# A chunk's product with the state ahead of the output projection of the chunk before, and small products in a group's waits

## The chip, the cores and the metric

The kernel runs on one core of one Trainium2 chip. A core has five engines, each with its own in-order queue: TensorE (PE in the profile; its weight loads are shown as PEld), VectorE (DVE), ScalarE (ACT), GpSimd (POOL) and SyncE (SP), which issues most DMAs. Matmuls write PSUM[...]. The metric is the time of one execution on the device, in microseconds (us); the median of several runs is compared.

## The reference, cut to what matters

```python
x = x + attn_a(layernorm(x))      # state-space mixer, 16 heads of 64, state 64
x = x + ffn(layernorm(x))
x = x + attn_b(layernorm(x))      # state-space mixer, 64 heads of 16, state 128
x = x + ffn(layernorm(x))         # the same ffn weights again
```

x is 4 x 1024 x 512, float32. Each mixer projects x to a gate z, to the channels h, B, C and to a step dt; h, B and C go through a causal convolution of four taps and a silu. Then, with a decay a = A*dt per head,

```python
state = exp(a_t) * state + (dt_t * h_t) outer B_t
y_t   = C_t . state + D * h_t
out   = rmsnorm_and_gate(y, z) @ out_proj
```

The kernel computes the recurrence by chunks of 128 positions. Inside a chunk y is a masked product, exp(segment sums of a) * (C B^T), times dt*h; what came before enters as C times the state at the chunk's start (`from_state`); then the state is brought on (`to_state`).

## The kernel before

The program is mixer A, ffn, mixer B, ffn, one behind the other. In a mixer the 4 x 1024 positions are 32 chunks of 128, eight to a batch row, and two chunks make a group (16 groups). A group's input projections, convolutions, gates and steps are the function `front`, a generator that yields after each of its 17 (A) or 18 (B) pieces: eight `gate` pieces (a `pz` product each) and nine (A) or ten (B) `convolve` pieces (a `pc` product each, ScalarE's `u` at L470 and three VectorE operations at L474 that read it). Two chunks of a group are worked off by `chunk` while the pieces of the next group's `front` are mixed in.

All four compute engines are under a manual schedule: instructions stand on each engine in the order in which the Python code issues them. The mixing is done by the loop at the end of `mixer`. Each `yield` of `chunk` names a time that is added to `due`; while `due` is positive, the next piece is issued and its own time (1.75 for a gate, 1.9 for a convolution) taken off. In the last group of a mixer there are no pieces. Functions put into `later_on` are issued after the next piece. The list `small` holds short TensorE steps (transposes, dt products, and the 13 steps of the next chunk's `prologue`: five in `sums_of`, eight in `turn`, two of which end in a VectorE product `hdt`, L713); `large` issues one of them after each big matmul, and `finish` issues what is left when a chunk needs it. `turn` also puts `skip` (four ScalarE scalings of h, L727) into `later_on`.

A chunk begins so, in program order:

1. `finish(f)`: what is left of its prologue (`misc`, `tph`; Gm, ea, Bt, hdt).
2. `fold` of the chunk before: two VectorE sums of its squares (L971, L972).
3. `decays(0)`: twelve short matmuls into four PSUM tiles `seg` (L789, L799), and four ScalarE exps that read them into `L` (L806).
4. `next(last, None)`, the first step of the `tail` of the chunk before: the output projection `pout` (eight products of 512 columns, L670) and the sum of squares `ssq` (L672), which needs `fold`. Its readers (`leave`: the copy at L679 and VectorE's `rs` at L680) go to `later_on`.
5. `from_state()`, unless the chunk is the first of its batch row: two products `po` (L847) of C with the state, and two VectorE products `yo` (L851) that read them.
6. On GpSimd `hdr` (L919) and the scaling of the state (L928), which waits for `po`.

Then come the weighing of `L` with Gm (`weigh`, L813), the transposes of `yo` into `py` (L860), the products of `L` with dt*h into `py` (`inner`, L829), `close_y` (L878 to L885) and `to_state` (`pst` L898, L907 or L909).

The profile counts a float32 product as two matmul instructions: `pout` is sixteen, `po` four. All the tiles that `mm(...)` makes (`pc`, `pz`, `pd`, `tpx`, `misc`, `tph`, `seg`, `pout`, `ssq`, `po`, `pst`, `pcs`) share the pool `p_mm`, seven PSUM buffers of one bank each; `py` has the eighth bank. A new tile waits until the last reader of the tile that had its buffer is done.

Of the kernel before, what the change touches and what calls it, by code (L numbers as in the profile page):

```python
# [72 lines left out]
def hybrid_kernel(  # L73
# [114 lines left out]
    def lay_constants():  # L188
        eye = ident.rearrange("p (r w) -> p r w", w=32)
        for i, at in enumerate(  # L190
            [slice(2 + h + 10 * lo, 7 + h + 10 * lo, 4) for lo in (0, 1) for h in range(HB)]
            + [slice(10 * lo, 10 * lo + 2) for lo in (0, 1)]
            + [slice(20, 21)]
        ):
            nc.vector.tensor_reduce(flags[:, i : i + 1], eye[:, :, at], mybir.AxisListType.XY, ALU.add)
        nc.vector.scalar_tensor_tensor(
            heads4, flags[:, HB : 2 * HB], 1.0 / LO_SCALE, heads4, ALU.mult, ALU.add
        )
        nc.vector.scalar_tensor_tensor(
            first2, flags[:, 2 * HB + 1 : 2 * HB + 2], 1.0 / LO_SCALE, first2, ALU.mult, ALU.add  # L200
        )
        for past in pasts:
            nc.vector.tensor_scalar_mul(
                past.rearrange("p t s -> p (t s)"), first2.to_broadcast([P, SETS * P]), -1.0
            )
            nc.vector.tensor_scalar(past[:, :, 64:], past[:, :, 64:], row20, None, ALU.add)

    def lay_flags(sets):
        for upto in sums:
            for t in sets:  # L210
                nc.vector.tensor_copy(upto[:, t], heads4.unsqueeze(2).to_broadcast([P, HB, P]))
                nc.vector.scalar_tensor_tensor(
                    upto[:, t, :, :64],
                    row20.unsqueeze(1).to_broadcast([P, HB, 64]),
                    MASKED,
                    upto[:, t, :, :64],
                    ALU.mult,
                    ALU.add,
                )
# [27 lines left out]
    def mixer(m, in_w, conv_w, conv_b, dt_bias, A_log, Dv, norm_w, out_w, src, dst, first, stats, last_steps={}):  # L247
# [14 lines left out]
        def state_at(half):  # L262
            return (slice(half * N, half * N + N), slice(0, 512)) if SH == 2 else (slice(0, N), slice(half * 512, half * 512 + 512))

        stack = ExitStack()
        with stack:
# [6 lines left out]
            def mm(name):  # L273
                return p_mm.tile([P, 512], F32, tag="mm", name=name)
# [69 lines left out]
            small = []  # L344
# [286 lines left out]
            def heads_of(ap):  # L631
                return ap.rearrange("p (h d) -> p h d", d=HD)

            def over_head(ap, parts, n):

                return ap.unsqueeze(2).to_broadcast([parts, n, HD])

            def packed(t, n):

                return t[:, n, 0::2, :]  # L640
# [122 lines left out]
            def chunk(f, c, following):  # L763
# [8 lines left out]
                last = state["tail"]  # L772
# [9 lines left out]
                def decays(t):  # L782

                    sg = [mm(f"seg_{tag}_{t}_{r}").rearrange("p (h l) -> p h l", h=HB) for r in range(4)]

                    for r in range(4):
                        for q in range(2):
                            at = slice(64 * q, 64 * q + 64)
                            nc.tensor.matmul(  # L789
                                sg[r][at, :, at],  # L790
                                ident16[at, at],
                                later[at, at].unsqueeze(1).to_broadcast([64, HB, 64]),
                                start=True,
                                stop=False,
                                skip_group_check=True,
                            )
                    for r in range(4):
                        rows = slice(32 * r, 32 * r + 21)
                        nc.tensor.matmul(  # L799
                            sg[r], past[rows, t, :], upto[rows, t], start=False, stop=True, skip_group_check=True  # L800
                        )
                    Ls = []
                    for r0 in (0, 2):
                        L = wk.tile([P, 2, HB, P], F32, tag="L", name=f"L_{tag}_{t}_{r0}", bufs=LB)
                        for r in range(2):
                            nc.scalar.activation(L[:, r], sg[r0 + r], AF.Exp)  # L806
                        Ls.append(L)
                    return Ls
# [32 lines left out]
                def from_state():  # L841

                    pos = []
                    for half in range(2):
                        rows, hsl = state_at(half)
                        po = mm(f"po_{tag}_{half}")
                        nc.tensor.matmul(po, Cc[rows, cols], state["S"][rows, hsl], start=True, stop=True)  # L847
                        pos.append(po)
                    for half, po in enumerate(pos):
                        tmp = wk.tile([P, 512], F32, tag="yo", name=f"yo_{tag}_{half}", bufs=2)  # L850
                        nc.vector.tensor_mul(  # L851
                            heads_of(tmp), heads_of(po), over_head(el[:, half * HALF : (half + 1) * HALF], P, HALF)
                        )
                        tmps.append(tmp)
# [56 lines left out]

                state.pop("fold", lambda: None)()
                L0 = decays(0)
                next(last, None)
                if not begin:
                    from_state()
                if not end:
                    hdr = wk.tile([P, E], F32, tag="hdr", name=f"hdr_{tag}")
                    nc.gpsimd.tensor_mul(  # L919
                        hdr.rearrange("p (n u d) -> p n u d", u=HC, d=HD),  # L920
                        packed(hdt, slice(0, NH // HC)),
                        er.rearrange("p (n u) -> p n u", u=HC).unsqueeze(3).to_broadcast([P, NH // HC, HC, HD]),
                    )
                    if begin:
                        Sp = wk.tile([P, SW], F32, tag="S", name=f"S_{tag}")
                    else:
                        Sp = state["S"]
                        nc.gpsimd.tensor_mul(heads_of(Sp), heads_of(Sp), over_head(et, P, NH // SH))  # L928
# [52 lines left out]
            with tc.manual_schedule(  # L981
                engines={
                    mybir.EngineType.PE,
                    mybir.EngineType.DVE,
                    mybir.EngineType.Activation,
                    mybir.EngineType.Pool,
                }
            ):
                fs = [Group(*groups[0]), Group(*groups[1])]
                for _ in norm(fs[0], None):  # L990
                    pass
                if first:
                    lay_constants()
                    lay_flags(range(TS))
                weighing = weigh_rows()
                for at, _ in enumerate(front(fs[0], fs[1])):
                    catch_up()
                    if at >= 6:
                        next(weighing, None)
                for _ in weighing:  # L1000
                    pass
                lay_sums(fs[0], 0)
                if first:
                    lay_flags(range(TS, SETS))
                for n in range(len(groups)):
                    if n + 2 < len(groups):
                        fs.append(Group(*groups[n + 2]))
                    f, ahead, behind = (fs + [None, None])[n : n + 3]
                    pieces = front(ahead, behind) if ahead is not None else iter(())
                    due = 0.0  # L1010
                    for c in range(GC):
                        following = (f, c + 1) if c + 1 < GC else (None if ahead is None else (ahead, 0))
                        for us in chunk(f, c, following):
                            due += us
                            while due > 0.0:
                                waiting, later_on[:] = later_on[:], []
                                piece = next(pieces, None)
                                for step in waiting:
                                    step()
                                if piece is None:  # L1020
                                    break
                                due -= piece
                            catch_up()
                    for _ in pieces:
                        catch_up()
                state.pop("fold")()
                for _ in state["tail"]:
                    catch_up()
# [438 lines left out]
```

## Time and profile before

| | |
|---|---|
| time, median of 3 runs | 3053.41 us (3053.19 to 3053.58) |
| the profiled execution: time, and its span | 3044.65 us, 3042.9 us |
| mean granted TensorE clock | 0.963 of full |
| mixer A, about | 60 to 1160 us: TensorE busy 1043.3 of 1100 |
| first ffn, about | 1160 to 1416 us |
| mixer B, about | 1416 to 2810 us: TensorE busy 1259.2 of 1394 |
| second ffn | the rest |
| busy share of the span | PE 91%, DVE 68%, ACT 41%, POOL 24% |

How to read it: one execution is traced. A row of the timeline is a start and a length in us, the engine, the line of the kernel, the operation, the tile written and the tiles read, the shape, and how many instructions the row merges; in brackets stands how long the engine idled before the row, and what ended that. A row of the waits is who waited for whom: us in total, times, the longest.

### The profile page before, as it was taken

What the parts mean: (1) busy time and instruction counts of PE and PEld (TensorE: products, weight loads), DVE (VectorE), ACT (ScalarE), POOL (GpSimd) and SP (SyncE); (2) the same over time, 40 slices, a digit from 0 to 9 for tenths busy, and PEclk for the clock granted to TensorE, in tenths of its full rate; (3) what the DMA queues carried; (4) which work ended last, traced back from release to release, by engine and by line L of the source; (5) the groups of instructions that cost most, each with busy time, mean ns of one, the idle gap of its engine ahead of it and who ended that gap; (6) DMA issues with size and microseconds to landing.
All of it is one profiled execution on the core that took longest, in us unless ns stands there. A gap on an engine that the chain in (4) does not pass through costs nothing. (4 is left out here: it accounts for less than half of the span.)

```text
span 3042.9 us, 46127 instructions
## 1 busy us (share of the span) xinstructions
PE 2767.9 (91%) x17156; PEld 1789.5 (59%) x17156; DVE 2081.7 (68%) x4417; ACT 1261.8 (41%) x2874; POOL 720.3 (24%) x839
## 2 busy tenths in 40 slices
PE   7999999999999988999999899999888888898986
PEld 5666666666666653456666666666555565564332
DVE  5667666766666662477777687776787777875368
ACT  3334433334333332355444444444444444443245
POOL 1222122122212221351111112212222222212057
PEclk8999999999999999999999999999999999998999
DMA  3000000000000015430000000000000000001423
GB/s 117 14 19 16 16 16 17 24 17 17 16 17 22 10 68 205 154 102 10 17 20 20 13 20 18 13 17 21 22 25 21 20 23 20 13 11 72 170 88 110
DMA packets 92959, 124.25 MB, mean 41 GB/s; under 512 B 38728, under 2 KB 42328, under 8 KB 92736
## 3 DMA queue, kind: packets, MB, share of 16 engines
q1 hardware_dynamic: 80960, 98.23, 10.0%
q10 hardware_dynamic: 9792, 16.82, 1.5%
q0 software_dynamic: 1984, 6.26, 0.6%
q8 instruction: 136, 2.23, 0.3%
q14 instruction: 87, 0.71, 0.1%
HBM read 84.54 MB, written 36.72 MB: 40 GB/s over the span
## 5 line engine op out<-in xcount | busy, mean ns | idle before, releaser
L347 PE MATMUL pc_b<-xnT_b,w_in_b 128*128 128x259 f32 x1280 | 355.7, 408 | 25.1 <-DVE S_b L909 21.9
L813 DVE TENSOR_TENSOR L_b<-L_b,Gm_b 128x1024 f32<-128x1024 f32 x256 | 308.7, 1247 | 2.9 <-ACT L_b L806 2.9
L347 PE MATMUL pz_a<-xnT_a,w_in_a 128*128 128x256 f32 x1024 | 296.5, 408 | 2.9 <-ACT Bt_a L756 2.3
L347 PE MATMUL pc_a<-xnT_a,w_in_a 128*128 128x259 f32 x1152 | 299.1, 394 | 0.0
L806 ACT ACTIVATE L_b<-seg_b 128x512 f32<-128x512 f32 x512 | 263.6, 603 | 74.0 <-PE seg_b L799 74.0
L347 PE MATMUL pz_b<-xnT_b,w_in_b 128*128 128x256 f32 x1024 | 291.4, 397 | 2.9 <-ACT xnT_b L436 2.9
L474 DVE SCALAR_TENSOR_TENSOR u_b<-pc_b,cw_b,u_b 128x256 f32<-128x256 f32 x480 | 231.5, 482 | 79.8 <-ACT u_b L470 68.3
L347 PEld LDWEIGHTS pc_b<-xnT_b,w_in_b 128*128 128x128 f32 x1280 | 229.3, 198 | 92.7 <-DVE S_b L909 25.4
L474 DVE SCALAR_TENSOR_TENSOR u_a<-pc_a,cw_a,u_a 128x256 f32<-128x256 f32 x432 | 208.2, 482 | 73.6 <-ACT u_a L470 63.3
L1205 PE MATMUL g_ps<-gw,xnT_f 128*128 128x512 f32 x512 | 246.9, 619 | 9.6 <-DMA gw<-in_L_ffn_gate_w 4.2
L829 PE MATMUL py_b<-L_b,hdt_b 128*32 128x128 f32 x4096 | 165.7, 299 | 97.6 <-DVE L_b L813 96.5
L670 PE MATMUL pout_a<-w_out_a,h_a 128*128 128x512 f32 x512 | 240.2, 613 | 0.0
L670 PE MATMUL pout_b<-w_out_b,h_b 128*128 128x512 f32 x512 | 235.7, 604 | 0.0
L347 PEld LDWEIGHTS pc_a<-xnT_a,w_in_a 128*128 128x128 f32 x1152 | 200.9, 190 | 58.5 <-DVE rs_a L685 11.4
L882 POOL TENSOR_TENSOR h_b<-h_b,z_b 128x256 f32<-128x256 f32 x128 | 90.8, 730 | 509.5 <-ACT sq_b L881 509.5
L347 PEld LDWEIGHTS pz_a<-xnT_a,w_in_a 128*128 128x128 f32 x1024 | 172.3, 195 | 55.0 <-ACT out_a L679 14.4
L347 PEld LDWEIGHTS pz_b<-xnT_b,w_in_b 128*128 128x128 f32 x1024 | 174.5, 194 | 48.8 <-issue 26.0
L829 PEld LDWEIGHTS py_b<-L_b,hdt_b 128*32 128x32 f32 x4096 | 112.6, 117 | 147.7 <-DVE L_b L813 60.5
L1205 PEld LDWEIGHTS g_ps<-gw,xnT_f 128*128 128x128 f32 x512 | 93.2, 196 | 122.1 <-issue 113.5
L881 ACT ACTIVATE sq_b<-h_b 128x256 f32<-128x256 f32 x128 | 47.9, 417 | 262.5 <-DVE h_b L878 262.5
L670 PEld LDWEIGHTS pout_a<-w_out_a,h_a 128*128 128x128 f32 x512 | 93.3, 192 | 100.1 <-issue 96.3
L670 PEld LDWEIGHTS pout_b<-w_out_b,h_b 128*128 128x128 f32 x512 | 92.3, 190 | 99.5 <-issue 95.7
(321 smaller groups left out, 4919.7 us busy)
## 6 DMA issues: line engine op xcount, KB each, us to landing
d<-in_L_ffn_d_w SPq DMA_DIRECT2D x4, 2048.0 KB
x_f<-xa SPq DMA_DIRECT2D x32, 256.0 KB
xb<-x_b ACTq DMA_DIRECT2D x32, 256.0 KB
x_f<-xb SPq DMA_DIRECT2D x32, 256.0 KB
x_a<-in_L_attn_a_x SPq DMA_DIRECT2D x30, 256.0 KB
xa<-x_a ACTq DMA_DIRECT2D x30, 256.0 KB
out<-x_f SPq DMA_DIRECT2D x22, 256.0 KB
xf<-x_f SPq DMA_DIRECT2D x20, 256.0 KB
```

Of the source, the lines that this page charges most:

```text
L347: nc.tensor.matmul(*args, **kw)
L474: nc.vector.scalar_tensor_tensor(u, ps[:, k : k + GT], cw[:, j, k : k + 1], u, ALU.mult, ALU.add)
L670: nc.tensor.matmul(pout, f.hs[e // 2][:, e % 2, cols], w_out[:, e, :], **on)
L806: nc.scalar.activation(L[:, r], sg[r0 + r], AF.Exp)
L813: nc.vector.tensor_mul(Lr, Lr, Gm.unsqueeze(1).to_broadcast([P, 2 * HB, P]))
L829: nc.tensor.matmul(py[cg * CT : (cg + 1) * CT, e % 4, :], hdt[:, h // HC, u : u + HC, :], Ls[half][:, r, hq, :], start=not started[cg], st ...
L881: nc.scalar.activation(sr, yh, AF.Square)
L882: nc.gpsimd.tensor_mul(yh, yh, zs[half * 2 + r][:, :, cols])
L1205: nc.tensor.matmul(ps, xnT[:, k, :], gw[:, k, :], start=(k == 0), stop=(k == KD - 1 and not bias_on_pe))
```

## The change

The call of `from_state` moves ahead of `next(last, None)`: on TensorE the chunk's four `po` instructions come ahead of `pout` and `ssq` of the chunk before, and their tiles are allocated ahead of those. On VectorE, ScalarE and GpSimd this move leaves the order as it is, since `tail`'s first step issues nothing there by itself.

In the loop at the end of `mixer`, when no piece is left, one step of `small` is issued at a time and 0.35 taken off `due`, until `due` is used up or `small` is empty. This can happen throughout the last group, and behind the last piece of any other.

```diff
                 state.pop("fold", lambda: None)()
                 L0 = decays(0)
-                next(last, None)
                 if not begin:
                     from_state()
+                next(last, None)
                 if not end:
                     hdr = wk.tile([P, E], F32, tag="hdr", name=f"hdr_{tag}")
...
                                 for step in waiting:
                                     step()
                                 if piece is None:
+
+                                    if small:
+                                        small.pop(0)()
+                                        due -= 0.35
+                                        continue
                                     break
                                 due -= piece
```

## The prediction

> **What bounds the kernel now.** I read the page first: TensorE is busy 91% of the span, the next engine 68%. An edit that moves TensorE work is therefore worth what it does to TensorE's own waits, and the second view to read is the table of waits. Call a group's first chunk even and its second odd; times are us from the span's start.
>
> ```profile
> PE 2767.9 (91%) x17156; PEld 1789.5 (59%) x17156; DVE 2081.7 (68%) x4417; ACT 1261.8 (41%) x2874; POOL 720.3 (24%) x839
> ```
> ```profile
> DVE yo_a L851 <- PE po_a L847: 124.7, 28, 8.6
> DVE yo_b L851 <- PE po_b L847: 122.0, 55, 7.4
> ...
> PE ssq_a L672 <- DVE sq_a L972: 28.8, 14, 2.7
> ```
>
> VectorE sits 247 us waiting for the product with the state (po), because po stands behind the output projection (pout, then ssq) on TensorE. That is what the edit moves. But VectorE's idle time counts only where TensorE later waits for VectorE. TensorE's own wait at this place is the third line: ssq waits for fold (L972) in 14 odd chunks of mixer A. The third view is one such chunk, engine by engine. TensorE:
>
> ```profile
> 512.38 0.40 PE L799 MATMUL seg_a<-upto,past 21*128 21x512 f16 x4
> 512.70 6.28 PE L670 MATMUL pout_a<-w_out_a,h_a 128*128 128x512 f32 x14
> 521.16 0.35 PE L672 MATMUL ssq_a<-ones,sq_a 128*128 128x1 f32 x2 [2.19 <-DVE sq_a L972]
> 521.38 1.10 PE L670 MATMUL pout_a<-w_out_a,h_a 128*128 128x512 f32 x2
> 522.32 0.28 PE L672 MATMUL ssq_a<-ones,sq_a 128*128 128x1 f32 x2
> 522.53 2.08 PE L847 MATMUL po_a<-S_a,Cc_a 64*128 64x512 f32 x4
> 524.53 3.09 PE L347 MATMUL pz_a<-xnT_a,w_in_a 128*128 128x256 f32 x10
> ```
>
> ScalarE and VectorE in the same stretch:
>
> ```profile
> 512.58 1.52 ACT L419 ACTIVATE xn_a<-x_a,mv_a 128x512 f32<-128x512 f32 x2 [2.69 <-DVE mv_a L417]
> ...
> 514.62 0.54 ACT L470 ACTIVATE u_a<-pc_a,cb_a,cw_a 128x256 f32<-128x256 f32 x1
> ...
> 517.07 2.04 ACT L806 ACTIVATE L_a<-seg_a 128x512 f32<-128x512 f32 x4
> ```
> ```profile
> 515.19 1.52 DVE L474 SCALAR_TENSOR_TENSOR u_a<-pc_a,cw_a,u_a 128x256 f32<-128x256 f32 x3 [2.26 <-ACT u_a L470]
> ```
>
> What to see: when TensorE reaches pout at 512.70, ScalarE is about 4 us behind. It has not yet read the last two convolution results, and it reads the four seg banks only from 517.07. Today pout covers that lag.
>
> **Why the order of allocation matters.** All these tiles live in a pool of seven PSUM buffers, handed out in the order in which they come free. At the start of an odd chunk of A the four segs hold four, and three convolution results the rest. In the program of before, pout takes the first one's buffer (read by 511.1), ssq the second one's (read until 515.19+1.52 = 516.71; it asks 7 us later, so this costs nothing), and po0, po1 take seg0's and seg1's. The edit swaps the claims: po0 takes the first, po1 the second, pout seg0's, ssq seg1's. TensorE runs in order, so everything behind po1 and pout (pout's 16 instructions, ssq, the gates) waits with them.
>
> **Odd chunks of A (15 with pieces left).** After the edit: po0 512.70 to 513.27 (half of the 1.13 us that an undisturbed po_a takes); po1 from 516.71 to 517.3; pout when the first exp ends, 517.07+0.58 = 517.65. pout and ssq take 7.41 without a wait (1101.00 to 1108.41 in another chunk), so the gates start at 525.06 against 524.53. The 2.19 wait on fold is gone (ssq now comes after 523, fold ended at 521.0), and two new waits of 3.4 and 0.4 have taken its place. The same lines in the other chunks: the first exp ends 3.9 us (3 chunks), 4.5 (1), 4.9 (7) or 5.4 (3) after the segs, 4.75 in the mean; the gates would start 4.75+7.45 = 12.2 after the segs, where they started 11.45 in the mean: 14 x 0.76 = 10.7, and 0.5 for the 15th, whose exp ends after 1.5. **+11.2 us** at unchanged clock.
>
> **The clock.** TensorE's granted clock falls to half after a poor stretch of 3.41 us:
>
> ```profile
> 447.40:450.81 3.41, 2.32 (x6) 0.76 (x4) 3.20 (x12) 2.36 (x5) 0.00 (x0) 1.00 0.00 0
> 450.81:454.23 3.42, 2.32 (x10) 1.20 (x10) 0.92 (x2) 0.58 (x1) 0.00 (x0) 1.00 0.00 0
> ```
> ```profile
> 519.09:522.50 3.41, 1.34 (x6) 0.89 (x6) 1.78 (x6) 0.02 (x1) 0.00 (x0) 1.00 0.00 0
> 522.50:525.92 3.42, 3.42 (x8) 1.69 (x9) 1.28 (x3) 0.58 (x1) 1.09 (x2) 0.50 0.00 0
> ```
>
> (Columns: length, then busy time of PE, PEld, DVE, ACT, POOL, the clock, DMA.) The same 2.18 us wait, split over two stretches (PE busy 2.32 of 3.41 in each), costs nothing; inside one (1.34) it halves the next. Seven of the 14 waits did so. The price is 0.95 up to po's end (chunks with and without, same wait) plus 0.66 on the next ten gate matmuls (3.09 against 2.43): 1.6 per halved stretch, and 3.0 where two follow each other (after the 2.73 waits). The new idle time is 3.4+0.4 within 4.4 us; however it falls, one stretch holds more than half idle. I take one halved stretch in ten chunks and two in four: 10x1.6+4x3.0 = 28. Of before's seven, the part up to po's end is in the 11.45 already; 7x0.66 = 4.6 is still to be taken off. **+23 us**. Bounds: none at all (-4.6) and two everywhere (+37).
>
> [...] The row above halves after 2.07 us idle of 3.41, so I follow the row.
>
> **Even chunks (12 in each mixer).** The exps follow the segs at once (first ended 0.6 after them in A, 0.3 in B), po finds the buffers of misc and of the first transposes free, and pout comes 1.1 (A) or 1.9 us (B) later, with its buffer free. TensorE executes the same work without a wait: 0. VectorE gets its two yo (0.69 each) earlier, but its next work waits for the dt projection behind pout: 0.
>
> **Odd chunks of B.** In nine the first exp ends at 0.6 or so: no new wait. VectorE saves 1.4 us, but z, ahead of L's weighing, waits for the gate's tanh within 0.2 us of where it ran: -0.5 in all. In the six where the last step of the first ffn is done too (from 2098 on), it ends 2.6 to 4.8 after the segs (3.7 in the mean) and po takes 1.9: pout starts 1.8 later than it could, against 0.3 to 1.7 of ssq wait removed. The gates come 1.1 later; TensorE's later waits on VectorE (0.5 to 1.5 each) give half back. 5 x 0.55 = 2.7 (the sixth already ran at half clock), and clock about 2.3 (1.8 us of idle falls into one stretch about 45% of the time). **+5**, between 0 and +12.
>
> **Small products at the end of a group.** Costs per chunk sum to 33.0 in A and the pieces to 31.1, so 1.9/0.35 gives six of the nine remaining prologue steps; in B 0.6 gives two. They stood next on TensorE anyway, so its order is unchanged: 0. In A four ScalarE scalings (0.31 each) now go ahead of the exps, by up to 0.9 us; whether pout's buffer is then seg0's or the second transpose's, I can't tell from the trace: 0 to 0.4 in 15 chunks. I take 0 (free within 0.5 of the segs by the transposes' row), +6 for the range.
>
> **Last groups.** Without pieces, the 13 steps now run in chunk 6 instead of as a burst ahead of chunk 7. They fall into waits such as this one:
>
> ```profile
> 1117.47 1.09 PE L860 MATMUL py_a<-ident,yo_a 128*128 128x128 f32 x4 [4.27 <-DVE h_a L878]
> ```
>
> The burst took 4.2 us in A (1120.39 to 1124.59, at half clock) and 2.0 in B. Against it, Gm (0.28) waits for its products ahead of the weighing of L on VectorE, up to 1 us, and the two hdt products (0.68 each) join its queue. I take **-3** for both, -6 to +1 for the range.
>
> **Queues.** Nothing moved issues a DMA: lay_sums stands ahead of the last yield and a Group's loads after it. SP is passed by nothing. On POOL the state's scaling (1.04 or 1.93) can start 7 us earlier, but POOL idled 218 and 192 us for it: 0.
>
> **Sum**: 11.2+23+5-0.5-3 = +36. The profiled execution took 3044.65 (span 3042.9), 8.8 under the median of the three runs; the sum is a difference on that execution, put on the median: 3053.4+36 = 3089.
>
> **Rivals.** (1) *The swap works as named; faster.* If pout finds a free buffer at +1.1 us, ssq meets fold 1.1 us later and each of the 14 waits shrinks by 1.1: -16; a wait of 1.1 halves no clock, up to -11 more; with the last groups, about 3028. It decides where pout's buffer comes free earlier than 1.1 us after the segs. For it: 28.8 us of ssq wait and 247 of VectorE are there. Against: L806 at 517.07. (2) *New waits, no loss of clock*: 11.2-4.6+2.7-3.5 = +6, 3059. Against: seven halvings after shorter waits. (3) *Worse*: two halved stretches in every chunk and the 0.4 in A's even ones: about 3115. (4) *Nothing*: gains and waits cancel within 0.2% (6 us, about what a measurement can tell from no change).
>
> **Chances**: main case (3072 to 3108) 0.70; rival 2 0.10, half of it within 0.2%; rival 1 0.10; rival 3 0.07; rival 4 0.03. Faster 0.10, same 0.08, slower 0.82. The range 3060 to 3112 leaves out rival 1, most of rival 3 and half of rival 2.
>
> **What would show it.** Right: the ssq wait of 28.8 us near 0; in A, TensorE waiting some 3 us at po or pout in 14 chunks, released by VectorE's u (L474) and ScalarE's L (L806); more half-clock stretches between 90 and 1080; yo's wait on po mostly gone without a gain. Wrong: pout directly behind po in A's odd chunks, or fewer half-clock stretches.

## The result, and the profile after

| | before | after |
|---|---|---|
| median of the runs compared | 3053.49 us (3053.19 to 3058.24, 4 runs) | 3096.69 us (3094.42 to 3099.74, 4 runs) |
| the profiled execution: time, span | 3044.65, 3042.9 | 3095.69, 3094.0 |
| mean granted TensorE clock | 0.963 | 0.953 |

The change makes the kernel slower: the ratio is 1.0138, with a 95% interval of 1.0121 to 1.0156, or 43 us.

The page after, engine by engine (busy us, share of the span, instructions):

```profile
PE 2813.3 (91%) x17156; PEld 1808.2 (58%) x17156; DVE 2086.6 (67%) x4417; ACT 1260.0 (41%) x2874; POOL 722.7 (23%) x839
```

The instruction counts are those of before. VectorE and ScalarE are as busy as they were (2081.7 and 1261.8 before); TensorE, with the same 17156 instructions, is busy 45 us longer (2767.9 before): not more work, but work at a lower clock, or work that no longer runs side by side. Both turn up below. The table of waits after (who waited for whom: total us, times, longest):

```profile
PE po_a L847 <- DVE u_a L474: 40.9, 14, 3.6
...
PE pout_b L670 <- ACT L_b L806: 10.1, 6, 2.0
```
```profile
DVE v_b L511 <- PE pd_b L503: 151.1, 32, 7.7
DVE v_a L511 <- PE pd_a L503: 148.0, 32, 7.0
...
DVE rs_a L680 <- PE ssq_a L672: 70.7, 18, 6.0
```

The row of `ssq` waiting for `fold`, 28.8 us, is gone, and so are VectorE's 247 us of waiting for `po`. In their place TensorE waits for VectorE's `u`, in 14 chunks again, and in mixer B for ScalarE's exps. VectorE's idle time was not saved, it moved to later waits for TensorE: at `v` (L511) for the dt projection 299 us in all, where it was 171 before, and at `rs` for `ssq`. An odd chunk of mixer A, TensorE:

```profile
538.29 0.40 PE L799 MATMUL seg_a<-upto,past 21*128 21x512 f16 x4
538.62 1.12 PE L847 MATMUL po_a<-S_a,Cc_a 64*128 64x512 f32 x2
542.77 1.09 PE L847 MATMUL po_a<-S_a,Cc_a 64*128 64x512 f32 x2 [3.04 <-DVE u_a L474]
543.80 7.97 PE L670 MATMUL pout_a<-w_out_a,h_a 128*128 128x512 f32 x14
551.61 0.28 PE L672 MATMUL ssq_a<-ones,sq_a 128*128 128x1 f32 x2
551.75 1.10 PE L670 MATMUL pout_a<-w_out_a,h_a 128*128 128x512 f32 x2
552.69 0.28 PE L672 MATMUL ssq_a<-ones,sq_a 128*128 128x1 f32 x2
552.83 2.41 PE L347 MATMUL pz_a<-xnT_a,w_in_a 128*128 128x256 f32 x10
```

VectorE and ScalarE in the same stretch:

```profile
541.11 1.52 DVE L474 SCALAR_TENSOR_TENSOR u_a<-pc_a,cw_a,u_a 128x256 f32<-128x256 f32 x3 [2.26 <-ACT u_a L470]
```
```profile
538.49 1.52 ACT L419 ACTIVATE xn_a<-x_a,mv_a 128x512 f32<-128x512 f32 x2 [2.69 <-DVE mv_a L417]
...
542.99 2.04 ACT L806 ACTIVATE L_a<-seg_a 128x512 f32<-128x512 f32 x4
```

What to see: po1 stands still until VectorE has read the second convolution result (541.11+1.52 = 542.63), and `pout`, which covered this lag before, stands behind it. ScalarE's lag is `xn` (L419) at the very start of the chunk: it waits 2.69 us for VectorE's `mv`, then takes 1.52, and everything behind it on ScalarE waits too. `pout`'s first row takes 7.97 us instead of the 6.28 of before: 3.41 us of it lie in a stretch at half clock (columns as in the prediction: length, busy PE, PEld, DVE, ACT, POOL, then the clock).

```profile
540.62:544.03 3.41, 1.25 (x3) 0.53 (x4) 2.78 (x7) 2.70 (x9) 0.01 (x1) 1.00 0.00 0
544.03:547.44 3.41, 3.41 (x5) 1.35 (x5) 3.24 (x9) 0.99 (x3) 1.08 (x2) 0.50 0.00 0
```

**Where the 51 us between the two spans lie.** The start of each chunk's first `seg`, after less before, read from both timelines:

| stretch | after less before, us |
|---|---|
| mixer A's start-up, up to its second chunk | +7.45 |
| mixer A's groups with pieces | +42.80 |
| mixer A's last group | -4.06 |
| first ffn | +2.66 |
| mixer B's groups with pieces, all from 2142 us on | +2.61 |
| mixer B's last group | -2.47 |
| second ffn | +2.05 |

In A's groups all of it lies in the steps out of odd chunks (+1.3 to +5.0 in 14 of them, +0.6 in the last one); the steps out of even chunks are -0.1 to 0. The 7.45 belong to the execution, not to the change: the first chunk took 38.2 us here, 31.6 before, and 31.5 in the trace of experiment 5, which issues the same instructions as the changed kernel up to there.

### The profile page after: what moved, and what is told of

It reads as the page before. It is cut to its first block, busy times and chain, and to the rows that moved or that the text cites. A ratio compares the mean times of both kernels' runs of the same rounds, so it can differ in the third digit from the quotient of the medians.

```text
span 3094.0 us, 46196 instructions
## 1 busy us (share of the span) xinstructions
PE 2813.3 (91%) x17156; PEld 1808.2 (58%) x17156; DVE 2086.6 (67%) x4417; ACT 1260.0 (41%) x2874; POOL 722.7 (23%) x839
## 5 line engine op out<-in xcount | busy, mean ns | idle before, releaser
L670 PE MATMUL pout_a<-w_out_a,h_a 128*128 128x512 f32 x512 | 263.6, 664 | 0.0
L670 PE MATMUL pout_b<-w_out_b,h_b 128*128 128x512 f32 x512 | 233.0, 599 | 10.1 <-ACT L_b L806 10.1
L670 PEld LDWEIGHTS pout_a<-w_out_a,h_a 128*128 128x128 f32 x512 | 102.9, 212 | 137.8 <-issue 133.8
```

Source lines behind the costliest of these rows:

```text
L670: nc.tensor.matmul(pout, f.hs[e // 2][:, e % 2, cols], w_out[:, e, :], **on)
```

## The experiments

Theory: the swap of claims makes po1 wait for `u` and `pout` for the exps, in A's odd chunks; the wait costs once as such and once more as clock. Rivals: the small products cost the time; the move costs in any chunk, whatever the buffers; the waits cost it all and the clock nothing.

**1. The move alone.** Only the diff's first hunk.

> The move of from_state alone, without the small steps in the loop. Buffer theory (the product takes the two buffers that come free first, the output projection has to wait for the first exp, and the idle time halves the clock): all of the loss is here, and what the small steps win in the last groups is missing, so 3096 to 3104 us, with the same waits of about 3 us at po in mixer A's odd chunks. Rival (the small steps cost, since they put four scalings ahead of the exps): under 3085 us.

Measured: 3097.49 us (3093.83 to 3105.63), ratio 1.0150 (1.0131 to 1.0170). The move is the whole loss.

**2. The small products alone.** Only the second hunk.

> The small steps in the loop alone, the order of product and output projection as before. Buffer theory: 3046 to 3053 us, a gain in the last group of each mixer of 2 to 4 us and nothing elsewhere. Rival (the small steps cost): over 3062 us.

Measured: 3051.15 us (3042.58 to 3070.57), ratio 0.9991 (0.9976 to 1.0007). They cost nothing. The first chunk of the last group is 2.7 us shorter in A and 1.8 in B (2.7 and 1.6 in the changed kernel).

**3. The move, but not in A's odd chunks.**

```diff
-                if not begin:
+                if not begin and not (m is MIX_A and c == 1):
                     from_state()
                 next(last, None)
+                if not begin and m is MIX_A and c == 1:
+                    from_state()
```

> The changed program, but in mixer A's second chunks the product stands behind the projection as before; it is moved in A's first chunks and in all of B, and the small steps are in. Buffer theory: first chunks cost nothing, B some 3 us, the small steps give 2, so 3054 (3048 to 3060). Rival (the move costs in every chunk, and the second chunks only show it): over 3065.

Measured: 3053.32 us (3042.93 to 3059.99), ratio 0.9985 (0.9973 to 0.9996). So even chunks and mixer B together cost no more than the small products gain, a few us at most, and the loss sits in 15 chunks.

**4. ScalarE's lag taken away.** In `norm`, three extra yields in mixer A: `xn` (L419) comes three pieces later and no longer falls ahead of the exps of an odd chunk. Once in the changed program, once in the program of before (line numbers from there on are 4 higher).

```diff
                     yield
                     yield
+                    if m is MIX_A:
+                        yield
+                        yield
+                        yield
                 xns = []
```

> The changed kernel, and in mixer A the normalized rows of the next group but one (xn, L419 on ScalarE) come three pieces later, so that ScalarE does not wait there for VectorE's mv while the last convolution results and the seg tiles of an odd chunk wait to be read. Buffer theory: without that lag the new waits at po and pout go to under 0.5 us, and so does most of the lost clock in mixer A; 3010 to 3025 us, and within 10 us of the same edit on the kernel before. Rival (the order itself costs, by VectorE's or GpSimd's work falling under the projection): about 43 us more than the same edit on the kernel before.

> The kernel before with the same edit of xn in mixer A. Both theories: the wait of ssq for fold (28.8 us) goes too, since VectorE's u no longer waits for ScalarE, and with it the seven half-clock stretches: 28.8 and some 15 us off, 3008 to 3018 us. If the lag has another cause than xn, it stays at 3053.

Measured: changed with it 3023.38 us (3017.7 to 3028.73), ratio 0.9904 (0.9885 to 0.9922); before with it 3005.02 us (2995.95 to 3010.77), ratio 0.9841 (0.9820 to 0.9862). The cause of the lag is confirmed: the first exp of an odd chunk now ends 2.3 us after the segs in the mean of the 14 chunks (4.75 before), and the distance between the two orders falls from 43 to 18 us. But it was expected within 10, so something was missing. The same odd chunk, first with `po` behind the projection, then with `po` ahead (both with the late `xn`):

```profile
492.34 6.28 PE L674 MATMUL pout_a<-w_out_a,h_a 128*128 128x512 f32 x14
...
499.74 1.13 PE L851 MATMUL po_a<-S_a,Cc_a 64*128 64x512 f32 x4
500.80 1.56 PE L347 MATMUL pz_a<-xnT_a,w_in_a 128*128 128x256 f32 x6
```
```profile
500.54 1.12 PE L851 MATMUL po_a<-S_a,Cc_a 64*128 64x512 f32 x2
502.21 1.09 PE L851 MATMUL po_a<-S_a,Cc_a 64*128 64x512 f32 x2 [0.55 <-DVE u_a L478]
503.23 6.28 PE L674 MATMUL pout_a<-w_out_a,h_a 128*128 128x512 f32 x14
```

The four `po` instructions take 1.06 us together (499.74 to 500.80), but the first two alone take 1.12. Each of the two products has 64 rows, where `pout` has 128 (`64*128` and `128*128` in the timeline). Issued back to back they run side by side: in an odd chunk of before the four instructions start two by two, at 313.5 and at 314.0, while `po`'s first two in the changed kernel start one behind the other, at 538.6 and at 539.2. With a wait between them the products run one after the other: 2.69 us from po0 to `pout` instead of 1.06, of which only 0.55 shows as idle. That is +1.6 in a typical odd chunk; with 0.5 in the chunks where the lag is shortest and 3.3 in two that met half clock, it makes up 22 us over mixer A's groups.

**5. The wait filled.** In the changed program, A's odd chunks issue po0's product three times over.

```diff
-                        nc.tensor.matmul(po, Cc[rows, cols], state["S"][rows, hsl], start=True, stop=True)
+                        for _ in range(3 if m is MIX_A and c == 1 and half == 0 and following is not None else 1):
+                            nc.tensor.matmul(po, Cc[rows, cols], state["S"][rows, hsl], start=True, stop=True)
```

> The changed program, but in mixer A's second chunks the first half of the product (po0) is computed three times over into the same buffer, the second and third time idle work that changes no value: 2.1 us of TensorE work in the wait of some 3 us for the second half. It orders nothing else differently. If the wait itself is what the change costs, the time stays at 3095 to 3100. If, as the trace says, only about 12 of the 43 us that mixer A lost are the waits and about 30 the halved clock behind them, TensorE is now busy in every 3.41-us stretch, the halved stretches between 90 and 1080 us go from 14 to 2 or fewer, and the time is 3060 to 3074.

Measured: 3088.79 us (3084.64 to 3098.27), ratio 1.0105 (1.0082 to 1.0128). Between the two expectations, and outside both: 11 of the 14 halvings were still there, though TensorE idled only 1.3 us per wait where before's three shortest waits, 1.17 to 1.18 us, halved nothing. Such a one, and the stretches behind it:

```profile
238.53:241.94 3.41, 2.30 (x6) 0.75 (x4) 1.39 (x4) 2.79 (x8) 0.00 (x0) 1.00 0.00 0
241.94:245.35 3.41, 3.20 (x4) 1.21 (x5) 3.27 (x9) 2.36 (x5) 1.01 (x2) 0.50 0.00 0
245.35:248.77 3.42, 3.42 (x5) 1.36 (x5) 3.21 (x11) 0.00 (x0) 0.08 (x2) 0.50 0.00 0
```

TensorE was busy 2.30 of 3.41 us, as in the pair of stretches that the prediction shows (2.32), and the next stretch was halved all the same; here the busy time was 64-row work. That is an observation; experiment 6 tests it.

**6. The wait filled with full rows, and with half rows of the same length.** Ahead of po0, three products into its buffer (2.7 us in all), overwritten by po0's own.

```diff
                         po = mm(f"po_{tag}_{half}")
+                        for _ in range(3 if m is MIX_A and c == 1 and half == 0 and following is not None else 0):
+                            nc.tensor.matmul(po, ident, w_out[:, 0, :], start=True, stop=True)
```

> As the run with the filled wait, but the idle work has all 128 rows: ahead of po0, three products of the identity with one block of the output weights into po0's buffer (0.9 us each, 2.7 in all; po0's own product overwrites them), in mixer A's second chunks. The run before filled the same wait with products of 64 rows and kept 11 of 14 halved stretches. If the clock follows TensorE's work weighted by the rows in use [...], a stretch with full rows stays at full clock: 3 or fewer of the 14 halved stretches are left between 90 and 1110 us, and the time falls by the clock's share, 25 to 32 us under the changed kernel: 3063 to 3073. If busy time counts whatever the rows, or the halving follows from something else than activity, it does no better than the filled wait: 3083 to 3092, 10 or more halved stretches.

The control has `ident[0:64, :]` and `w_out[0:64, 0, :]` instead.

> The kernel with the 128-row filler once more, with the same three idle products of the same length at the same place, but over 64 of the 128 rows (rows 0 to 63 of the identity and of the output weights). Waits and busy time are the same as there; only the rows in use differ. If the clock follows the work weighted by its rows, the halved stretches of mixer A come back (9 or more between 90 and 1110 us, where the 128-row filler had none), and the time is 3080 to 3092. If the clock follows busy time alone (the filled wait of 64 rows kept 1.3 us idle, this one 0.3), there are 2 or fewer and the time is 3061 to 3069.

Measured: full rows 3065.26 us (3060.91 to 3068.92), ratio 1.0040 (1.0021 to 1.0059); half rows 3063.72 us (3060.3 to 3074.94), ratio 1.0028 (1.0011 to 1.0046). Mixer A's groups (90 to 1110 us) after, and with the full-row filler:

```profile
90.00:1110.00 1020.00, 970.38 (x5034) 646.20 (x5035) 667.15 (x1564) 374.33 (x938) 206.97 (x271) 0.96 0.05 17
```
```profile
90.00:1110.00 1020.00, 1006.54 (x5286) 671.35 (x5286) 691.03 (x1626) 388.66 (x973) 217.19 (x282) 1.00 0.05 17
```

With full rows not one stretch is halved, though every wait is still there for the chunk: `pout` starts as late after the segs as in the chunks of the changed program where po1 ran at full clock (5.1 us in the chunk shown above, and the same there with the filler). This separates wait from clock. The step out of A's last odd chunk, which has no wait to fill, is 2.1 us longer with the filler than without; over the 14 others the kernel with the filler gains 34.3 us on the changed one and is 7.9 behind before. So the halvings of the changed kernel cost 34.3 us, 0.46 per us at half clock (34.3/75.1).

That is not yet the clock's part in the loss, because before had halvings too, 30.7 us at half clock in these groups. At the same price they cost 14 us, an estimate. Of A's 42.8 us the clock then makes up about 20 (34.3-14.0), and the waits, with the two products of `po` no longer side by side, about 22 (7.9+14.0). The starts of the gates say the same: 12.3 us after the segs in the mean of the 14 chunks with the filler, against 10.7 in before without its halvings (8.3 to `ssq` in the mean, and 2.4 from there on in the chunks without one); 14 x 1.6 = 22.

The control refuted what was expected of rows: with half rows only two halvings are left, not nine or more. What it shows instead, in two of its stretches and those behind them:

```profile
384.11:387.52 3.41, 2.39 (x6) 0.63 (x4) 2.55 (x6) 2.69 (x8) 0.00 (x0) 1.00 0.00 0
387.52:390.94 3.42, 3.42 (x5) 1.51 (x5) 3.21 (x10) 1.27 (x3) 1.38 (x2) 0.50 0.00 0
244.16:247.58 3.42, 2.99 (x7) 0.95 (x6) 1.56 (x4) 2.71 (x8) 0.00 (x0) 1.00 0.00 0
247.58:250.99 3.41, 3.38 (x8) 1.46 (x9) 3.24 (x9) 2.28 (x5) 1.09 (x2) 1.00 0.02 5
```

Behind 2.39 us of 64-row work the next stretch was halved, behind 2.99 it was not. Rows made a difference, two halvings with half rows against none with full ones, but a smaller one than I had expected.

**7. The product between projection and sum of squares.** The changed program with another order: `pout`, then `po`, then `ssq`.

```diff
                 for e in range(KE):
                     nc.tensor.matmul(pout, ...)
-                    if e >= KE - 2:
-                        nc.tensor.matmul(ssq[:, 0:1], ...)
+                yield
+                for e in (KE - 2, KE - 1):
+                    nc.tensor.matmul(ssq[:, 0:1], ...)
...
+                next(last, None)
                 if not begin:
                     from_state()
                 next(last, None)
```

> The changed program, but with the product with the state between the output projection and its sum of squares (pout, po, ssq), in every chunk. Buffer theory: pout takes the first convolution result's buffer again and covers ScalarE's lag, po takes buffers that were read long before it asks, and its 1.06 us lie in the wait of the sum of squares for fold. 14 waits of 2.06 us in the mean (28.8 in the view of before) shrink by 1.06 each: -14.8; waits of 1.0 halve no clock, so of the seven halved stretches of mixer A up to 7 x 1.6 = 11 come back; the small steps give 2. From 3053: 3025 to 3037. Rival (VectorE sets the pace of the chunk; what the sum of squares no longer waits comes back as a wait for L or for the gates): 3046 to 3054.

Measured: 3008.7 us (3007.48 to 3010.78), ratio 0.9839 (0.9825 to 0.9854), 16 us better than the best of what was expected. `ssq`'s wait for `fold`:

```profile
PE ssq_a L673 <- DVE sq_a L974: 6.6, 10, 1.6
```

28.8 us became 6.6, not 14. The expectation moved `ssq` back by `po`'s 1.06 alone; but `ssq` also comes behind the last two instructions of `pout`, another 1.1 us that stood behind the wait before. One odd chunk with the new order:

```profile
504.19 7.13 PE L670 MATMUL pout_a<-w_out_a,h_a 128*128 128x512 f32 x16
511.25 1.13 PE L848 MATMUL po_a<-S_a,Cc_a 64*128 64x512 f32 x4
512.63 0.58 PE L673 MATMUL ssq_a<-ones,sq_a 128*128 128x1 f32 x4 [0.25 <-DVE sq_a L974]
```

`pout` starts right behind the segs, and `po` is again one row of four. Halved time between 90 and 1110 us is 13.6 us, where it was 30.7 before and 75.1 after. Of the distance to the kernel with the small products alone (42 us), mixer A's groups have 32 and mixer B's 8; B's part was not taken apart.

**8. What beats both.** The late `xn` with the small products, and the same with the order of 7.

> The program of before with the normalization of mixer A's next group three pieces later (as in the run before) and with the small products in the last groups; the product is not moved. The two gains lie in different stretches, so they add: 3005 - 2 = 3003 (2998 to 3007). If the small products cost time in the groups with pieces, over 3008.

> The late normalization in mixer A, the small products, and the product between projection and sum of squares, together. In mixer A the late normalization has already taken nearly all of the wait for fold away, so the order adds under 2 there; in mixer B it took about 8 us off in the run with the order alone. Theory: 3000.6 - 8 = 2992 (2987 to 2997). Rival (the waits taken away in B are the same ones in both, or come back at L): 2999 to 3004.

Measured: 3000.57 us (2992.09 to 3002.99), ratio 0.9807 (0.9788 to 0.9827), and 2992.38 us (2990.32 to 2995.02), ratio 0.9793 (0.9779 to 0.9808). The last is the fastest kernel here, 2% under before. The median lies where the theory put it (2992), but what the order adds to the other two is not settled: the medians are 8 us apart, yet they were measured on different occasions, their runs overlap, and the profiled spans (2990.4 and 2989.6) hardly differ. By chunk the two traces agree with the theory in part: the order gains 6.4 us over mixer B's groups, loses 1.7 over A's, and A's start-up happened to take 3.3 longer in the second trace.

## Why the prediction was right, point by point

The predicted 3089 us lies 8 under the measured 3096.69, inside the range, for the reasons given. The 8 us are no sum of large errors that cancel: A's groups came out at 42.8 where 34.6 was predicted, B's odd chunks 1.9 under their figure and the last groups 1.2 over theirs. By its steps:

- **Order of allocation, odd chunks of A.** Right in the main: po1 starts 4.15 us after po0, released by `u` (4.0 in the prediction), the `fold` wait is gone, and there is a wait of about 3 us in 14 chunks. The waits at full clock, less the halvings of before, were put at 11.2-4.6 = 6.6; with the full-row filler they are 7.9 in 14 chunks, and 0.6 in the 15th from the changed program. One detail was wrong: the prediction gave po1 0.57 us, half of what the four take together, but alone it takes 1.03 (542.77 to 543.80), so in A it is po1's end and not the exp that lets `pout` start. That is 1.6 of the 1.9 us: the gates start 12.3 after the segs in the mean, predicted 12.2. The prediction's "at unchanged clock" holds for the changed kernel only; the 11.45 that it compares with contains halvings of before.
- **The clock.** The largest term, and the one that was mis-sized: 28 for the changed kernel's halvings, 34.3 measured. All 14 chunks had one, as predicted, but eight had two stretches in a row where four were taken: 75.1 us at half clock instead of 61.4 (18 stretches of 3.41). The price per halved us was right (28/61.4 = 0.46, and 34.3/75.1 = 0.46). In all eight, and in none of the other six, po1 falls into the halved stretch, 1.29 to 2.04 us of 64-row work at half clock, as here (1.31), and the next stretch is halved too. (In four of the eight TensorE also idled 1.1 to 1.5 us in that stretch; which of the two did it there is open.)

```profile
755.65:759.07 3.42, 0.39 (x2) 0.30 (x2) 1.97 (x5) 2.71 (x9) 0.00 (x0) 1.00 0.00 0
759.07:762.48 3.41, 3.41 (x5) 1.14 (x4) 3.20 (x9) 1.87 (x4) 1.18 (x2) 0.50 0.01 2
762.48:765.89 3.41, 3.41 (x5) 1.34 (x5) 3.24 (x10) 0.00 (x0) 0.00 (x0) 0.50 0.00 0
```

- **The row that halved after 2.07 us idle of 3.41.** Without loss of clock A was worth +7 (11.2-4.6); by the row, +35. A lost 42.8, and only the kernel without a halved stretch came near the first figure (7.9 in the 14 chunks). The row decided rightly.
- **Even chunks: 0.** Right, also with ScalarE's scalings ahead of the exps (-0.1 to 0 per chunk; `pout` has no wait there).
- **Odd chunks of B: +5 less 0.5.** Measured +2.6, all in the groups with the ffn's last step; `pout` waits for the exps six times, 10.1 us in all.
- **Last groups: -3.** 6.5 us are gained in the mixers, and the ffn behind each gives 2.7 and 2.1 back: -1.8. Why the ffns take longer stays open.
- **Rivals.** Rival 1, the faster one, fell at the point that it named itself: `pout`'s buffer is not free at 1.1 us. Its aim was sound, as experiment 7 shows: `po` can fill the wait for `fold`, if it does not stand ahead of `pout`. Rival 2, without loss of clock, is about what the full-row filler makes of the kernel: predicted 3059, measured 3065.

## What to carry to other kernels

Before work is moved ahead in an in-order queue, ask whose buffers it claims and what it then stands in front of: a long product that needs nothing is the cover for the engines that lag, and a short one placed ahead of it uncovers the lag. Look first for a place behind the cover and ahead of the next wait; here that turned a loss of 1.4% into a gain of 1.6%. And price a new TensorE wait twice, once as time and once as clock, for the program before as well as for the one after: of the 43 us that mixer A's groups lost here, about 20 were clock, by the estimate of experiment 6.

## What the runs showed of the hardware

The clock was granted in stretches of 3.41 us or whole multiples of it, at 1.00 or 0.50: in the trace of before 46 stretches at each. Read over mixer A's groups, three things stood out that I had not expected.

- With full-row work, busy 1.61 of 3.41 us was followed by a halved stretch (the first pair of rows, of before), and busy 1.81 was not (the second, of the kernel of experiment 3):

```profile
99.25:102.66 3.41, 1.61 (x6) 0.71 (x5) 2.51 (x9) 0.77 (x2) 0.00 (x0) 1.00 0.01 2
102.66:106.08 3.42, 3.42 (x8) 1.18 (x6) 0.00 (x0) 0.58 (x1) 0.00 (x0) 0.50 0.00 0
```
```profile
934.01:937.43 3.42, 1.81 (x5) 0.51 (x3) 3.21 (x12) 2.36 (x5) 0.00 (x0) 1.00 0.00 0
937.43:940.84 3.41, 2.28 (x10) 1.20 (x10) 0.95 (x2) 0.59 (x1) 0.00 (x0) 1.00 0.00 0
```

- With 64-row work, a halved stretch followed 2.39 us of it and none followed 2.99 (the control of experiment 6), so 2.39 us of 64 rows did worse than 1.81 us of full ones. No run varied rows alone between these figures. In experiment 7, a halved stretch followed 1.82 us of work, 0.9 of it a row of four `po` side by side, where none had followed the 1.81 of full rows.

```profile
373.77:377.18 3.41, 1.82 (x10) 0.99 (x9) 3.31 (x7) 0.45 (x1) 1.38 (x2) 1.00 0.00 0
377.18:380.60 3.42, 3.42 (x9) 2.60 (x8) 1.95 (x12) 0.00 (x0) 0.70 (x2) 0.50 0.02 5
```

- A stretch at half clock was followed by a second one after 0.47 us idle, where 1.6 us idle at full clock (the row with 1.81 busy) was followed by none. Before and the changed kernel have 21 stretches in these groups that were halved behind one at full clock. In the ten that a second followed, TensorE idled 0.47 us or more, or spent 1.29 us or more on 64-row work alone; in the other eleven it did neither. In experiment 5, 3.20 us busy of 3.41, with 1.97 of it 64-row work, was followed by a second halved stretch.
